# Keys and queries of a head pair by seven half-size products, with their copies behind the exponentials

## The chip, the cores and the metric

The kernel runs on one core of one Trainium2 chip. The metric is the device time of one execution in microseconds (us). All data are float32. The core's engines are TensorE (PE; its weight loads are shown apart as PEld), VectorE (DVE), ScalarE (ACT), GpSimd (POOL) and SyncE (SP, which here only issues DMAs). Each engine takes its instructions in the order of the program; semaphores hold an instruction back until what it needs is there.

## The reference, cut to what matters

Four sequences of 1024 rows and 256 features go through four layers, each added to its input:

```
x = x + attention_a(layernorm(x))      # layer 1: 16 heads of 64
x = x + ffn(layernorm(x))              # 256 -> 1024, exact gelu, -> 256
x = x + attention_b(layernorm(x))      # low-rank q, k, v and rotary embedding
x = x + ffn(layernorm(x))              # the same weights again
```

In layer 1, with `h = layernorm(x)` of one sequence, every head has

```
q, k, v = h @ Wq, h @ Wk, h @ Wv                 # 256 -> 64 each
scores  = (q @ k.T) / (64 * 64 * 16)
out     = softmax(scores) @ v                    # then out @ WO, summed over the heads
```

## The kernel before

**Pairs and steps.** Two heads make a pair (128 columns of a weight), so a sequence has 8 pairs and layer 1 has 32. A pair has 8 steps; a step handles 128 query rows of both heads against all 1024 keys. Layer 1 therefore has 256 steps, numbered `s`. Everything is written out by hand in the order in which the engines shall meet it: one pass of the loop in `steps_with` (L342 to L365) emits work of several steps, and `pieces` is a table that says after which pass other work (the projections of the next pair, layer norms, weight loads) is emitted. A key that ends in a half (`s - EARLY`) stands in the middle of the pass, between the two halves of a step's exponentials; a whole key stands at its end.

**One pass `s`.** In this order: `invert(s)` takes the reciprocal of the softmax sums (DVE, L268) and spreads it into an extra column block of `p` (ACT, L269). `scores(s + 1)` makes the scores of the next step: eight matmuls into two tiles `sc`, one for each half `j`, and the matmuls alternate between the tiles (L247). `exponentials(s + 1, j)` finds the row maximum of one `sc` tile (DVE, L258) and takes the exponential (ACT, L260); this is what reads `sc`. `turn(s)` transposes the probabilities in blocks of 32 (DVE, L280), and `send` carries the blocks to their places by DMA (L304, eleven by SP and five by POOL for two steps).

Passes come in twos. In a pass with odd `s` the kernel also multiplies the probabilities of two earlier steps with the values: `weigh` (PE, L313), then `take` copies the result (ACT, L323) and scales it (POOL, L325). In a pass with even `s` `project` multiplies that with the output weights (PE, L176 with `wo`, in `mm`), copies the sum out of PSUM (ACT, `got`, L335) and adds it to `x` (POOL, L337). Below, an even pass is called a projecting pass, an odd one a weighing pass, and both together a beat.

**The next pair's keys and queries.** While one pair's steps run, the next pair's are made. `qk` (L744 to L758) is called four times in a pair, once in each projecting pass, at a half key: for keys and queries, for each half of the sequence, it multiplies 128 weight columns with 512 columns of the transposed `hT`, over two chunks of the 256 features (`paired`: two column halves of PE for each chunk, so four matmuls a call, L176 with `hT,w`), and ACT copies the bank out (L756, L758), also between the step's two exponentials. `values` (L185, copied by L769) is called at the end of a projecting pass.

**PSUM.** It has eight banks. The pool `ps_sc` has three tiles of two banks, handed out in turn; in layer 1 only `scores` takes from it. The pool `ps_mm` has two tiles of one bank, taken alternately by everything else through `group`:

```
    ps_sc = ctx.enter_context(tc.tile_pool(name="ps_sc", bufs=3, space=PSUM))
    ps_mm = ctx.enter_context(tc.tile_pool(name="ps_mm", bufs=1, space=PSUM))
```

**Elsewhere.** Both feed-forward layers already multiply blocks by seven products instead of eight (`up_seven`, `down_seven`): sums of blocks are made first, the seven products are taken, and their results are added up. `w2_sb` (1 MB), and the rotary tables `cos_sb` and `sin_sb` (0.5 MB each), are loaded at the start on POOL's queue and stay in SBUF. `rows.measure` takes mean and variance of 128 rows on DVE (L135, L136); 24 such are spread over the steps 4 to 27, and the feed-forward layer's first eight over the steps 236 to 243.

Of the kernel before, what the change touches and what calls it, by code (L numbers as in the profile page):

```python
# [15 lines left out]
P = 128  # L16
# [3 lines left out]
NC = D // P  # L20
# [14 lines left out]
EPS = 1e-5  # L35
EARLY = 0.5
PLACES = {
    (3, 0): (0, 1), (3, 10): (2,), (3, 11): (3,), (3, 12): (4,), (3, 13): (5,),
# [10 lines left out]
def hybrid_block_kernel(  # L49
# [24 lines left out]
    pp, tp, ptp, otp, tmp = pool("p", 2), pool("T", 2), pool("pT", 2), pool("oT", 1), pool("tmp", 1)  # L74
    lowp, highp, xnp, rp = pool("low", 2), pool("high", 1), pool("xn", 1), pool("rope", 1)
    qkp, vp, wp, wop = pool("qk", 2), pool("v", 2), pool("wp", 2), pool("wo", 2)

# [15 lines left out]
    w1_sb = const.tile([P, NC, F], F32, name="w1_sb")  # L93
    w2_sb = const.tile([P, NF, D], F32, name="w2_sb")
    b2_sb = const.tile([P, D], F32, name="b2_sb")
    wd_sb = const.tile([P, 2, NC, P], F32, name="wd_sb")
    cos_sb = const.tile([P, S], F32, name="cos_sb")
    sin_sb = const.tile([P, S], F32, name="sin_sb")

    def load_rest():  # L100
        for b in range(1, B):
            nc.sync.dma_start(xs[b], xv[b])
        nc.gpsimd.dma_start(w1_sb, w1.rearrange("(c p) f -> p c f", p=P))
        nc.gpsimd.dma_start(w2_sb, w2.rearrange("(c p) d -> p c d", p=P))
        nc.gpsimd.dma_start(b2_sb, b2.partition_broadcast(P))
        for i, w in enumerate((wdq, wdkv)):
            nc.gpsimd.dma_start(wd_sb[:, i], w.rearrange("(c p) r -> p c r", p=P))
        for j in range(2):
            nc.gpsimd.dma_start(cos_sb[j * DH : (j + 1) * DH, :], rope_cos)
            nc.gpsimd.dma_start(sin_sb[j * DH : (j + 1) * DH, :], rope_sin)  # L110
        nc.gpsimd.dma_start(b1_sb, b1.rearrange("(c p) -> p c", p=P))
        nc.gpsimd.dma_start(lns_sb, ln_s.rearrange("(c p) -> p c", p=P))
        nc.gpsimd.dma_start(lnb_sb, ln_b.rearrange("(c p) -> p c", p=P))


# [41 lines left out]

    def transposed(dst, src, c, affine=None):

        tr = group(TQ, P)  # L160
        for t in range(TQ):
            nc.tensor.transpose(tr[:, t, :], src[:, t, ts(c, P)], ident)  # L162
        trf = tr.rearrange("p t q -> p (t q)")
        if affine is None:
            nc.scalar.copy(dst[:, c, :], trf)  # L165
        else:
            nc.scalar.activation(
                dst[:, c, :], trf, AF.Identity,
                scale=affine[0][:, c : c + 1], bias=affine[1][:, c : c + 1],
            )  # L170
# [18 lines left out]

    def attention(prep_batch, prep_pair, wo, loader, lead, kept):  # L190

# [135 lines left out]
        def project(h):  # L327
            g, t0 = divmod(HB * h, NT)
            b, pr = pairs[g]
            po = group(HB, D)  # L330
            for t in range(HB):
                paired(po[:, t, :], [(oT[h][:, t], [wos[g][:, t]] * 2)])
            oT.pop(h)
            got = tmp.tile([P, HB, D], F32, tag="tmp", name="got")
            nc.scalar.copy(got, po)  # L335
            xd = xs[b][:, t0 : t0 + HB, :]
            nc.gpsimd.tensor_add(xd, xd, got)  # L337

        def steps_with(others):
            for k, f in others:  # L340
                pieces.setdefault(k, []).append(f)
            for s in range(-1, n + LAG + 1):  # L342
                h, part = divmod(s - LAG, HB)
                ahead = 0 <= s + 1 < n
                if 0 <= s < n:
                    invert(s)
# [4 lines left out]
                if part == 1 and 0 <= h < n // HB:  # L351
                    project(h)
                if ahead:
# [5 lines left out]
                if ahead:  # L359
                    exponentials(s + 1, 1)  # L360
                if part == 0 and 0 <= h < n // HB:
                    take(h)
                if 0 <= s < n:
                    turn(s)
# [30 lines left out]
    def ffn(rows, store):  # L395
# [31 lines left out]
        def weights():  # L427
# [5 lines left out]
            parts["w1"] = (s1, w1_sb[:, 0, :m], w1_sb[:, 1, :m], w1_sb[:, 1, m:])  # L433
            lo, hi = w2_sb[:, :hf], w2_sb[:, hf:]
            parts["w2"] = (s2, lo[:, :, :P], hi[:, :, :P], hi[:, :, P:])
            v = nc.vector
            work = four([s1[:, i] for i in range(4)], w1_sb[:, 0, :m], w1_sb[:, 1, :m], w1_sb[:, 0, m:], w1_sb[:, 1, m:], [v] * 4)
            work += other([s2[:, i] for i in range(4)], lo[:, :, :P], lo[:, :, P:], hi[:, :, :P], hi[:, :, P:], [nc.gpsimd] * 4)
            for f in work:
# [114 lines left out]
        def down_seven(n, hook):  # L554
            b, qb = blocks[n]
            t4, b11, b21, b22 = parts["w2"]
            s, g = sums.pop(n), gT[n]
            a11, a12, a22 = g[:, :hf, :half], g[:, hf:, :half], g[:, hf:, half:]
            pairs = {
                1: (a11, b11), 2: (a12, b21), 3: (s[:, 3], b22), 4: (a22, t4[:, 3]),  # L560
                5: (s[:, 0], t4[:, 0]), 6: (s[:, 1], t4[:, 1]), 7: (s[:, 2], t4[:, 2]),
            }
# [4 lines left out]
            def product(bank, k, first):  # L567
                l, r = pairs[k]
                product_of(bank, lambda t, f: l[:, f, ts(t, P)], lambda f: r[:, f], first, hf)

# [39 lines left out]
        def down(n, t):  # L610
# [3 lines left out]
            for f in range(NF):  # L614
                nc.tensor.matmul(  # L615
                    po[n][:, t % 2, :], gT[n][:, f, ts(t, P)], w2_sb[:, f, :],
                    start=(f == 0), stop=(f == NF - 1),
                )
# [9 lines left out]
    def ffn_between(rows, store, n_steps, nxt=None, prologue=(), ramp=None):  # L628
# [11 lines left out]
        ends += [(n - 1 + (0, 0, 0, 1, 2, 2, 3, 3)[f], lambda f=f: up(0, f)) for f in range(NF)]  # L640
        ends += [(n, lambda: normed(1))]
        ends += [(n + 1, lambda m=m, t=t: rows.measure(m, t)) for m in range(2, 6) for t in range(TQ)]
        ends += [(n + 2, lambda: rows.finish[1]()), (n + 2, weights), (n + 3, lambda: turned(1))]
        ends += [(n + 3, lambda: row_sums(1)), (n + 4, lambda: down(0, 0))]

        def rest():
# [3 lines left out]
            for m in range(1, last + 1):  # L650
# [11 lines left out]
                if m == 1:  # L662
                    for i in range(2 * TQ):
                        when(2 + i, lambda i=i: rows.measure(6 + i // TQ, i % TQ))
                if nxt and m >= 2:
                    for t in range(TQ):
# [38 lines left out]
    def layer_a():  # L705

        scale_a = 1.0 / (DH * DH * H)
        hTs = {}
        rows = Rows("a", (blocks[:1], blocks[1:2], blocks[2:]))

        def batch_a(b):
            work = []
            for qb in range(NQB):
# [12 lines left out]
                def turned(c, b=b, k=k, qb=qb):  # L726
                    if c == 0:
                        p, tag = ((lowp, "low"), (highp, f"high{b % 2}"))[qb]
                        hTs[b, qb] = p.tile([P, NC, QB], F32, tag=tag, name="hT")
                    transposed(hTs[b, qb], k["xn"], c)  # L730

                work += [(10 * qb + t, lambda t=t, f=straight: f(t)) for t in range(TQ)]
                work += [(10 * qb + 6 + 2 * c, lambda c=c, f=turned: f(c)) for c in range(NC)]
            return work

        def pair_a(b, pr):
# [9 lines left out]
            def qk(i, qb):  # L746
# [6 lines left out]
                ])  # L753
                dst = made[name][:, ts(qb, QB)]
                if i == 0:
                    nc.scalar.mul(dst, pq, scale_a)  # L756
                else:
                    nc.scalar.copy(dst, pq)  # L758

            def values(m):  # L760
# [3 lines left out]
                for t in range(4):  # L764
# [3 lines left out]
                    ])  # L768
                nc.scalar.copy(made["v"][:, ts(m, 4), :], pv)  # L769

            work = [(4 - 4 * i + 2 * qb - EARLY, lambda i=i, qb=qb: qk(i, qb)) for i in (1, 0) for qb in range(NQB)]
            work += [(6 + 2 * m, lambda m=m: values(m)) for m in range(NT // 2)]
            return {name: lambda name=name: made[name] for name in ("qT", "kT", "v")}, load, work


        later = [(4 + i, lambda i=i: rows.measure(2 + i // TQ, i % TQ)) for i in range(6 * TQ)]
        later += [(4 + 6 * TQ, lambda: rows.finish[2]())]
        first, steps = attention(batch_a, pair_a, wo_a, nc.gpsimd, lead=3, kept=0)
        loads, xn, pair = first[:2], first[2:14], first[14:]
# [11 lines left out]
        first = loads + [lambda: measured(0)] + xn[:4] + [lambda: measured(1), ready] + xn[4:6] + pair[:1]  # L791
        first += xn[6:] + pair[1:3]
        later += [((-1, 0, 0, 1, 1)[i], f) for i, f in enumerate(pair[3:])]
# [3 lines left out]
    def layer_b(rows):  # L797
# [4 lines left out]
        def batch_b(b):  # L802
            work = []
            for qb in range(NQB):
# [33 lines left out]
                work += [(16 * qb - 12 + t, lambda t=t, f=second: f(t)) for t in range(TQ)]  # L838
                work += [(16 * qb - 8 + 2 * c - EARLY, lambda c=c, f=turned: f(c)) for c in range(NC)]
                work += [(16 * qb + 2 * m, lambda m=m, f=down: f(m)) for m in range(2)]  # L840
            return work

        def pair_b(b, pr):
# [23 lines left out]
            def rotate(i, qb):  # L867

                straight, other = made[i, qb], turned.pop((i, qb))
                nc.gpsimd.tensor_mul(straight, straight, cos_sb[:, ts(qb, QB)])  # L870
                nc.gpsimd.tensor_mul(other, other, sin_sb[:, ts(qb, QB)])  # L871
                nc.gpsimd.tensor_add(straight, straight, other)
# [19 lines left out]

        return attention(batch_b, pair_b, wo_b, nc.sync, lead=5, kept=1)

# [74 lines left out]
```

## Time and profile before

| what | value |
| --- | --- |
| median of 3 runs | 3253.63 us (3250.37 to 3256.33) |
| the profiled execution | 3250.15 us, its span 3248.4 us |
| granted clock of TensorE, mean | 0.996 |
| scores of layer 1 | 22.56 to 1412.5 us of the span; its last `weigh` until 1447.8 us |
| scores of layer 3 | 1661.0 to 3002.7 us; the feed-forward layers lie behind the two, overlapping their ends |

The profile is one execution as the hardware profiler saw it. Busy shares are averages over these four stages, so layer 1 is read by itself, from a stretch of steady steps. Times in a timeline are us from the start of the span; a number in square brackets is how long the engine was idle before an instruction, with what it waited for.

### The profile page before, as it was taken

Reading aid. Unit: us, or ns where it says so; the run is one execution under the profiler, and the core shown is the slowest. Engines: PE = TensorE matmul, PEld = TensorE weight load, DVE = VectorE, ACT = ScalarE, POOL = GpSimd, SP = SyncE. Lnnn points to the kernel's source line nnn. Section 1 sums busy time; section 2 is a strip of 40 time slices with the busy share of each in tenths; the row PEclk is TensorE's granted clock in tenths of the full one; section 3 lists DMA queues with packets and bytes.
Section 4 is the critical chain, followed back from the end, with each engine's and each line's share of the span. In section 5 each row is a group of like instructions: output and inputs, shape, how many; then the busy total and the mean of one; then the engine's idle time right before and its main releaser. Section 6 shows DMA issues by size and latency. Waiting matters only on the chain.

```text
span 3248.4 us, 128967 instructions
## 1 busy us (share of the span) xinstructions
PE 3164.4 (97%) x53648; PEld 2092.2 (64%) x53648; DVE 2723.5 (84%) x2686; ACT 2137.9 (66%) x4400; POOL 2002.1 (62%) x2782
## 2 busy tenths in 40 slices
PE   8999999999999999999999999999999999999999
PEld 4666666666666666668866566666666666655688
DVE  7988888888888888966569989998999999999554
ACT  5666666666666666655447777777778777777542
POOL 4544545455444545442249889899899889886311
PEclk9999999999999999999999999999999999999999
DMA  8888888888888888850029889988989899988200
GB/s 228 217 224 215 224 224 228 217 219 222 221 217 225 219 231 223 221 150 1 4 74 244 225 228 243 242 237 236 246 243 243 234 240 246 238 235 221 57 20 27
DMA packets 244709, 642.29 MB, mean 198 GB/s; under 512 B 74304, under 2 KB 102976, under 8 KB 244128
## 3 DMA queue, kind: packets, MB, share of 16 engines
q1 hardware_dynamic: 161104, 397.60, 48.0%
q0 software_dynamic: 83024, 236.44, 26.0%
q8 instruction: 426, 6.98, 1.0%
q14 instruction: 155, 1.27, 0.1%
HBM read 43.39 MB, written 4.19 MB: 15 GB/s over the span
## 4 chain that ended last, share of the span: by engine, by line
PE 69%; SPq 12%; DMA 6%; DVE 5%; ACT 4%; issue 3%; POOL 1%; DVEq 0%; ACTq 0%; POOLq 0%
PE sc L247 20%; PE mm L313 19%; PE mm L176 15%; SPq L304 11%; DMA pT<-T 5%; PE pw L495 4%; PE mm L185 4%; PE mm L495 3%; PE mm L615 2%; DVE T L280 2%; DVE nmax L258 1%; ACT p L260 1%; PE ph L604 1%; ACT gT L529 1%; PE mm L162 1%
## 5 line engine op out<-in xcount | busy, mean ns | idle before, releaser
L258 DVE TENSOR_REDUCE nmax<-sc 128x1 f32<-128x1024 f32 x1024 | 1204.5, 1218 | 214.3 <-PE sc L247 211.3
L260 ACT ACTIVATE p<-sc,nmax 128x1024 f32<-128x1024 f32 x1024 | 1145.3, 1119 | 322.3 <-DVE nmax L258 322.2
L280 DVE STREAM_TRANSPOSE T<-p 128x2176 f32<-128x2176 f32 x512 | 1247.3, 2436 | 48.4 <-DMA pT<-T 18.4
L247 PE MATMUL sc<-kT,qT 64*64 64x512 f32 x8192 | 1082.5, 598 | 11.9 <-ACT p L260 10.3
L313 PEld LDWEIGHTS mm<-pT,v 64*64 64x64 f32 x32768 | 949.5, 133 | 140.7 <-issue 98.5
L313 PE MATMUL mm<-pT,v 64*64 64x128 f32 x32768 | 983.0, 269 | 9.6 <-issue 8.5
L304 POOL DMA_DIRECT2D pT<-T x1280 | 629.6, 499 | 125.5 <-PE sc L247 57.7
L325 POOL TENSOR_TENSOR oT<-oT,pT 128x256 f32<-128x256 f32 x256 | 187.0, 730 | 696.3 <-ACT oT L323 623.0
L247 PEld LDWEIGHTS sc<-kT,qT 64*64 64x64 f32 x8192 | 332.8, 133 | 401.6 <-issue 274.5
L337 POOL TENSOR_TENSOR x<-x,got 128x512 f32<-128x512 f32 x256 | 331.0, 1293 | 25.8 <-ACT got L335 22.0
L335 ACT COPY got<-mm 128x512 f32<-128x512 f32 x256 | 150.0, 586 | 281.8 <-PE mm L176 281.8
L176 PE MATMUL mm<-wo,oT 128*64 128x256 f32 x2048 | 279.9, 394 | 24.1 <-POOL oT L325 22.8
L176 PEld LDWEIGHTS mm<-wo,oT 128*64 128x64 f32 x2048 | 124.9, 136 | 273.2 <-POOL oT L325 226.5
L269 ACT COPY p<-total 128x128 f32<-128x128 f32 x512 | 151.9, 297 | 198.6 <-DVE total L268 192.4
L176 PE MATMUL mm<-hT,w 128*64 128x512 f32 x1024 | 243.4, 597 | 0.9 <-ACT hT L165 0.9
L260 ACT ACTIVATION_READ_ACCUMULATOR p<-sc,nmax 128x1 f32 x1024 | 205.2, 200 | 0.0
L185 PEld LDWEIGHTS mm<-w,hT 128*64 128x64 f32 x4096 | 140.9, 138 | 71.3 <-issue 69.4
L871 POOL TENSOR_TENSOR turned<-turned,sin_sb 128x512 f32<-128x512 f32 x128 | 163.8, 1279 | 0.0
L409 POOL TENSOR_TENSOR x<-x,b_sb 128x256 f32<-128x256 f32 x64 | 48.8, 777 | 170.6 <-ACT xn L156 170.6
L296 ACT COPY pT<-T 32x1088 f32<-32x1088 f32 x128 | 140.3, 1096 | 4.9 <-DMA pT<-T 1.1
L185 PE MATMUL mm<-w,hT 128*64 128x64 f32 x4096 | 140.9, 222 | 0.2 <-ACT kT L758 0.2
L176 PEld LDWEIGHTS mm<-hT,w 128*64 128x64 f32 x1024 | 73.3, 138 | 96.8 <-issue 75.0
(145 smaller groups left out, 2928.5 us busy)
## 6 DMA issues: line engine op xcount, KB each, us to landing
pT<-T SPq DMA_DIRECT2D x2688, 136.0 KB, 4.7
pT<-T POOLq DMA_DIRECT2D x1280, 136.0 KB, 4.7
turned<-kT POOLq DMA_DIRECT2D x128, 128.0 KB, 3.4
turned<-qT POOLq DMA_DIRECT2D x128, 128.0 KB, 3.5
w<-in_wqkv_a POOLq DMA_DIRECT2D x96, 128.0 KB, 6.0
wo<-in_wo_a POOLq DMA_DIRECT2D x32, 128.0 KB, 5.4
wo<-in_wo_a POOLq DMA_DIRECT2D x64, 64.0 KB, 5.5
wo<-in_wo_b SPq DMA_DIRECT2D x32, 128.0 KB, 4.0
```

What stands on the lines that cost most here:

```text
L176: nc.tensor.matmul(out[ts(j, DH)], lhsT[:, ts(j, DH)], rhs[j], start=(first and i == 0), stop=(last and i == len(parts) - 1),)
L185: nc.tensor.matmul(out[ts(j, DH)], lhsT, rhs[:, ts(j, DH)], start=(i == 0), stop=(i == len(parts) - 1),)
L247: nc.tensor.matmul(sc[s, j][ts(half, DH), ts(m, 512)], qT()[rows, ts(2 * qs + half, DH)], kT()[rows, ts(m, 512)], start=True, stop=True,)
L258: nc.vector.tensor_reduce(nmax, sc[s, j], AX.X, ALU.max, negate=True)
L260: nc.scalar.activation(probs[s][:, :NK2, ts(j, 2), :], sc.pop((s, j)).rearrange("p (k c i) -> p k c i", c=2, i=SQ), AF.Exp, bias=nmax, acc ...
L280: nc.vector.transpose(T[h][:, :, q, :, :].rearrange("p c k i -> p k c i"), probs.pop(s))
L304: engine.dma_start(pT[h][ts(c, SQ), a], T[h][ts(a, SQ), c])
L313: nc.tensor.matmul(av[h][q][ts(j ^ q, DH)], v[ts(j, DH), k, :], pT[h][ts(j, DH), :, q, k, :], start=(k == 0), stop=(k == NK2 - 1),)
L325: nc.gpsimd.tensor_mul(parts, parts, pT.pop(h)[:, :, :, NK2, :])
L337: nc.gpsimd.tensor_add(xd, xd, got)
L495: nc.tensor.matmul(bank[:, t, : right(k).shape[-1]], left(t, k), right(k), start=(first and t == 0 and k == 0), stop=(k == n_k - 1), skip_ ...
L871: nc.gpsimd.tensor_mul(other, other, sin_sb[:, ts(qb, QB)])
```

## The change

The keys and queries of a pair, for one sequence, are a product of 2 by 2 blocks: queries and keys as rows, the two feature chunks as the inner index, the two halves of the sequence as columns. That took eight block products; now it takes seven (numbered 1 to 7), for 31 of the 32 pairs. The first pair still calls `qk`.

Before the products, POOL makes four sums of weight blocks of a pair (`weight_sums`, at a key two passes before the pair's first products), and DVE makes four differences of blocks of `hT` once for each sequence (`row_sums`: for the first sequence ahead of the first step, for the other three in the passes 21 to 24 after their table's zero). The products are taken in the four projecting passes in the groups (1, 6), (7, 5), (4, 2) and (3), each group into one `ps_sc` tile of two banks, tag `sc`. At the end of the pass ACT copies one product of the group, and DVE and POOL add: DVE one sum out of PSUM in each of the first three groups, POOL none, two, one and one sums in SBUF.

With `late=True` (layer 1 only) `project` returns its copy and addition, and they are emitted after the step's second exponential, unless more than one piece of that pass takes a `ps_mm` bank (`banked`). The scale of the scores moves into the copy of `hT` (`root`), and `values` undoes it. To make room in SBUF, `w2` is loaded in four parts at the end of layer 1 and the rotary tables in the first feed-forward layer, both on SP's queue; their space (pool `tail`) serves the sums before.

```diff
@@ def project(h):
-            got = tmp.tile([P, HB, D], F32, tag="tmp", name="got")
-            nc.scalar.copy(got, po)
-            xd = xs[b][:, t0 : t0 + HB, :]
-            nc.gpsimd.tensor_add(xd, xd, got)
+            def added():
+                got = tmp.tile([P, HB, D], F32, tag="tmp", name="got")
+                nc.scalar.copy(got, po)
+                xd = xs[b][:, t0 : t0 + HB, :]
+                nc.gpsimd.tensor_add(xd, xd, got)
+
+            return added
@@ one pass
                 if part == 1 and 0 <= h < n // HB:
-                    project(h)
+                    added = project(h)
+                    both = pieces.get(s - EARLY, []) + pieces.get(s, [])
+                    if not late or sum(getattr(f, "banks", 0) for f in both) > 1:
+                        added()
+                        added = None
...
                 if ahead:
                     exponentials(s + 1, 1)
+                if added:
+                    added()
@@ def pair_a(b, pr):
+            def weight_sums():
+
+                s = made["s"] = tail.tile([P, 4, P], F32, tag="w20", name="ws")
+                (q0, q1), (k0, k1) = [[made["w"][:, i, c, :] for c in range(NC)] for i in range(2)]
+                nc.gpsimd.tensor_add(s[:, 0], k0, k1)
+                nc.gpsimd.tensor_sub(s[:, 1], s[:, 0], q0)
+                nc.gpsimd.tensor_sub(s[:, 2], q0, k0)
+                nc.gpsimd.tensor_sub(s[:, 3], q1, s[:, 1])
+
+            def products(which):
+
+
+                w, s, t = made["w"], made["s"], [sums[b][k // 2][:, k % 2] for k in range(4)]
+                h = [[hTs[b, qb][:, c, :] for qb in range(NQB)] for c in range(NC)]
+                sides = {
+                    1: (w[:, 0, 0], h[0][0]), 2: (w[:, 0, 1], h[1][0]), 3: (s[:, 3], h[1][1]),
+                    4: (w[:, 1, 1], t[3]), 5: (s[:, 0], t[0]), 6: (s[:, 1], t[1]), 7: (s[:, 2], t[2]),
+                }
+                both = ps_sc.tile([P, 2, QB], F32, tag="sc", name="pw")
+                for i, k in enumerate(which):
+                    made[k] = both[:, i]
+                for k in which:
+                    l, r = sides[k]
+                    paired(made[k], [(l, [r] * 2)])
+
+            def added(which):
+
+
+                q, k = made.get("qT"), made.get("kT")
+                if which == (1, 6):
+                    made["u2"] = tail.tile([P, QB], F32, tag="w22", name="u2")
+                    nc.vector.tensor_add(made["u2"], made[6], made["x1"])
+                elif which == (7, 5):
+                    made["u3"] = tail.tile([P, QB], F32, tag="w23", name="u3")
+                    nc.vector.tensor_add(made["u3"], made[7], made["u2"])
+                    nc.gpsimd.tensor_add(made["u2"], made["u2"], k[:, QB:])
+                    nc.gpsimd.tensor_add(k[:, QB:], k[:, QB:], made["u3"])
+                elif which == (4, 2):
+                    nc.vector.tensor_add(k[:, :QB], made[4], made["u3"])
+                    nc.gpsimd.tensor_add(q[:, :QB], q[:, :QB], made["x1"])
+                else:
+                    nc.gpsimd.tensor_add(q[:, QB:], q[:, QB:], made["u2"])
...
-            work = [(4 - 4 * i + 2 * qb - EARLY, lambda i=i, qb=qb: qk(i, qb)) for i in (1, 0) for qb in range(NQB)]
-            work += [(6 + 2 * m, lambda m=m: values(m)) for m in range(NT // 2)]
+            if b == 0 and pr == 0:
+                work = [(0, lambda i=i, qb=qb: qk(i, qb)) for i in (1, 0) for qb in range(NQB)]
+            else:
+                work = [(-2, weight_sums)]
+                for i, which in enumerate(((1, 6), (7, 5), (4, 2), (3,))):
+                    work += [(2 * i - EARLY, lambda which=which: products(which))]
+                    work += [(2 * i, lambda which=which: copied(which))]
+                    work += [(2 * i, lambda which=which: added(which))]
+            work += [(6 + 2 * m, banked(lambda m=m: values(m))) for m in range(NT // 2)]
```

The function `copied` (not shown) holds the ACT copy of each group: of product 1 into `x1`, of 5 into the keys, of 2 and of 3 into the queries.

## The prediction

> **What bounds the kernel now.** I read the page first, then layer 1 by itself, because the busy shares are averages over four stages.
>
> ```profile
> PE 3164.4 (97%) x53648; PEld 2092.2 (64%) x53648; DVE 2723.5 (84%) x2686; ACT 2137.9 (66%) x4400; POOL 2002.1 (62%) x2782
> ```
>
> PE is busy almost throughout. Whether that means "full" is seen in the chain that ended last, for a stretch of layer 1 (start, us, what): one beat, from the end of one projecting pass's scores to the end of the next one's.
>
> ```profile
> 608.01 2.73 PE mm L176 x16
> 610.74 0.93 PE mm L185 x32
> 611.67 1.88 PE sc L247 x16
> 613.55 3.49 PE mm L313 x128
> 617.04 1.72 PE sc L247 x16
> ```
>
> Nothing but PE stands in it, without a gap: 2.73 + 0.93 + 1.88 + 3.49 + 1.72 = 10.75 us. (L176 holds the projection and `qk` together.) So layer 1 is bound by PE's matmuls, and taking some away can help, if nothing else is close behind. What is close behind is seen in the timeline of the same beat.
>
> ```profile
> 608.06 2.36 DVE L258 TENSOR_REDUCE nmax<-sc 128x1 f32<-128x1024 f32 x2 [0.46 <-PE sc L247]
> 608.85 1.89 PE L176 MATMUL mm<-hT,w 128*64 128x512 f32 x8
> 609.12 0.59 ACT L335 COPY got<-mm 128x512 f32<-128x512 f32 x1 [1.19 <-PE mm L176]
> 609.61 1.12 ACT L260 ACTIVATE p<-sc,nmax 128x1024 f32<-128x1024 f32 x1
> 610.33 2.44 DVE L280 STREAM_TRANSPOSE T<-p 128x2176 f32<-128x2176 f32 x1
> 611.27 1.12 ACT L260 ACTIVATE p<-sc,nmax 128x1024 f32<-128x1024 f32 x1
> 611.60 0.21 PEld L247 LDWEIGHTS sc<-kT,qT 64*64 64x64 f32 x8
> 613.60 2.36 DVE L258 TENSOR_REDUCE nmax<-sc 128x1 f32<-128x1024 f32 x2 [0.78 <-PE sc L247]
> ...
> 615.99 1.12 ACT L260 ACTIVATE p<-sc,nmax 128x1024 f32<-128x1024 f32 x1
> ...
> 617.00 0.19 ACT L260 ACTIVATION_READ_ACCUMULATOR p<-sc,nmax 128x1 f32 x1
> ```
>
> DVE idles only 0.46 + 0.78 = 1.24 us in a beat. And the scores of the weighing pass start at 611.60, while the projecting pass's second exponential still runs (to 612.39). They may, because with three `sc` tiles in turn they take the third tile and the first.
>
> **Part 1, the matmul removed.** Of 2.73 us in the chain the projection has 0.85 (the weighing pass ends the same way), `qk` 1.88: four matmuls, that is two block products of 0.94 us. Groups (1, 6), (7, 5), (4, 2) stay at 1.88; group (3) saves 0.94. If PE's work set the time: 31 pairs × 0.94 = 29 us less. A rule of the Trainium skill speaks otherwise ("Perfetto Trace Analysis", Identifying the Most-Contended Engine: judge TensorE's headroom by its weight loads, not by matmul busy time): by it PEld's 64% would leave room and this term would be worth about 0. The gapless chain is against that, so I go by the row.
>
> **Part 2, the tile taken from the scores.** A group of products takes one of the three `sc` tiles in every projecting pass. Then the turn is: scores X, Y; products Z; scores of the weighing pass X, Y again. These now need *both* exponentials of the step just before. The copies of `got` and of the product move behind the second exponential, which brings that one forward; I work out when it ends. In the weighing pass, where no copy stands between, the reductions start at 613.60 and the second exponential's last instruction ends at 617.00 + 0.19 = 617.19, so 3.59 after. For reductions at 608.06: 611.65. The release costs little more; the layer's first steps show it, where the scores do wait:
>
> ```profile
> 26.83 0.19 ACT L260 ACTIVATION_READ_ACCUMULATOR p<-sc,nmax 128x1 f32 x1
> 26.95 1.11 ACT L260 ACTIVATE p<-sc,nmax 128x1024 f32<-128x1024 f32 x1
> 27.07 0.28 PEld L247 LDWEIGHTS sc<-kT,qT 64*64 64x64 f32 x8 [0.58 <-ACT p L260]
> ...
> 29.06 2.35 DVE L258 TENSOR_REDUCE nmax<-sc 128x1 f32<-128x1024 f32 x2 [0.70 <-PE sc L247]
> ```
>
> Released at 27.02, weights at 27.07, and the next reduction 1.99 after that, as in the free case (611.60 to 613.60). The first matmul, which goes into the first tile, had run alone before, and that saved nothing. So in the beat above the scores can go on at 611.70 instead of 611.60, and the loop closes on itself: reductions to release 3.64, release to the next reductions 1.99, weighing and scores to the next projecting pass's reductions (613.60 to 618.81) 5.21: 10.84 us a beat against 10.75. PE's own work no longer enters. In the group (3) beat PE comes 0.94 earlier and waits 0.94 + 0.09. The whole gain of part 1 is spent, and 31 × 4 beats × 0.09 = **+11 us** come on top.
>
> **Part 3, DVE's additions.** Three a pair; the nearest row is the feed-forward's sum out of PSUM:
>
> ```profile
> L540 DVE TENSOR_TENSOR u<-pw,u 128x512 f32<-128x512 f32 x14 | 9.5, 675 | 0.7
> ```
>
> 0.68 us each, placed after the transpose. In the order of instructions each waits for ACT's product copy too. ACT: exponential to 611.65, then `got`, `v`, the copy (0.59, 0.37, 0.59, each starting some 0.1 before the last one's shown end): to about 613.0. The addition then runs to 613.75, the reciprocal to 613.85, and the reductions start there instead of at 613.70. Behind them come the exponentials, `take` (POOL at 617.64 + 0.25, 0.73 long, to 618.62) and the projection, which starts at 618.69 today. It just fits: +0.02 a beat, **+3 us**. If ACT's copies follow more slowly by 0.2, it is 0.2 on 93 beats, 19 us.
>
> **Part 4, beats where DVE has no room.** 32 measures (385 + 182 ns) fall two to a beat into 16 beats: 1.13 of the slack of 1.24. With an addition, 0.68 + 1.13 less the new slack of 1.24 + 0.09 = 1.33 is 0.5 us over in three quarters of them: +6. The 12 block differences of the later sequences come two to a beat in six beats, 0.69 each (the feed-forward's 128x512 difference of weights took 693 ns): up to 0.7 over, +3. Together **+9**, from 3 to 20. The Trainium skill ("SBUF — State Buffer", Who interferes with whom) says that a DVE instruction with both inputs in SBUF and a GpSimd one that reads SBUF block each other for a whole instruction. A similar sum that took 1100 ns instead of 680 agrees with something like it; with a full block of 1.29 us for each of the 12 the term would be some 15 us larger. The additions of part 3 have one input in PSUM and are outside that rule.
>
> **Part 5, POOL.** Additions of 128x512 take 1.29 us (L337), 128x256 0.73 (L325), so 128x128 about 0.45 by that slope (estimate). Group (7, 5): `got` 612.3 to 613.6, two additions to 616.2, before `take` at 617.6: hidden. The tight beat is group (3): `got` 613.6, one addition 614.9, four weight sums 616.7, then the three `wo` loads (0.58 + 2 × 0.53) 618.3, and only then `take`, to 619.1: the projection starts 0.3 late, of which 0.1 was waiting anyway: 31 × 0.2 = **+6**, from 0 to 10. Group (4, 2) has one addition and three `w` loads (2.2 us) to 617.1: hidden by 0.5.
>
> **Part 6, the ends.** In the first six steps, where reductions come every 4.65 us (DVE sets the pace), three additions come in: +2. The first sequence's four differences fall into DVE's idle 11.49 us before its first reduction: 0. 2 MB fewer loads in the first 30 us: 0, as PE waits there for ACT and DVE, not for loads; at most 2.1 MB at the 293 GB/s of that window, −7. The later loads (eight issues on SP's queue, about 1 us each) delay transfers that lag five steps: 0. The scale in the copies (598 ns with, 587 without) and POOL's split weight sums in the feed-forward layers: 0. **+2**, from −7 to 5.
>
> **Sum.** 11 + 3 + 9 + 6 + 2 = +31 on the profiled execution's 3250.15: 3281. That execution lies 3.5 under the median of the runs, within their spread of 6; I say 3281. One measurement of this kernel can tell about 0.2% (6.5 us) from no change.
>
> **Rivals.**
>
> *The gain comes through (faster).* The scores' wait decides only if the second exponential is released later than PE arrives. If it ended 0.94 us earlier in the group (3) beats than worked out (by 610.66), 29 us come off, less the small terms (10): 3231. For it: ACT has 34% idle. Against it: 608.06 + 3.59 is two reductions and one exponential in a row, without any idle time to take out. I give it 0.10.
>
> *All fits, no change.* Parts 3 to 5 vanish in slack, the start gives a few us back: 11 − 7 = +4, 3254. It needs the projection's start, today 0.31 after POOL's end, to absorb everything. 0.15.
>
> *DVE becomes the bound.* If addition, copy wait and semaphores take 0.3 more per beat than the 1.33 of slack, in all 93 beats with an addition: +28 on top, 3309. For it: 9.5 busy of 10.75 before, 10.2 after. 0.20.
>
> *The forecast*, waits a little longer than PE's work: 0.55.
>
> The products are taken in 31 of 32 pairs by the order of instructions, so "it does nothing" is no case.
>
> **Range.** Low 3252, with the waits at 0.09 and nearly all else hidden; high 3314, with DVE as the bound. The faster case and the tails are left out. Faster 0.10; same 0.13, since the case of no change reaches a little past the bound; slower the rest, 0.77.
>
> **What would show it.** Right: in layer 1 PE idle before L266 (the scores' new line), released by ACT `p`, about 1 us once a pair; DVE's idle time before the reductions nearly gone; beats of 10.85 to 11.1. Part 5 is right if the projection after group (3) waits for POOL `oT`. Wrong: beats of 10.75 with one of 9.8 in each pair; or PE waiting for something else, such as the weights' sums or DMA.

## The result, and the profile after

The changed kernel takes 3268.02 us (median of 20 runs, 3261.26 to 3279.43) against 3253.43 (20 runs, 3247.26 to 3262.66). The ratio is 1.0044, 95% interval 1.0036 to 1.0052: slower by 14.6 us. Forecast were 3281 and a range from 3252 to 3314. The profiled execution took 3261.26 us with a span of 3259.5, that is 11.1 more than before's; the runs and traces of one kernel differ by several us, so the loss is located by layer below.

The page's first part: the shares of PE and ACT stay, DVE and POOL gain the sums.

```profile
PE 3171.1 (97%) x53524; PEld 2129.3 (65%) x53524; DVE 2800.6 (86%) x2795; ACT 2132.6 (65%) x4400; POOL 2206.5 (68%) x3033
```

Now the timeline of two beats of layer 1. The first has group (4, 2), the second group (3); L277 are the reductions, L279 the exponentials, L266 the scores, L356 is `got`, L862 DVE's addition.

```profile
625.09 2.35 DVE L277 TENSOR_REDUCE nmax<-sc 128x1 f32<-128x1024 f32 x2 [0.46 <-PE sc L266]
626.34 1.11 ACT L279 ACTIVATE p<-sc,nmax 128x1024 f32<-128x1024 f32 x1 [1.39 <-DVE nmax L277]
...
628.49 0.19 ACT L279 ACTIVATION_READ_ACCUMULATOR p<-sc,nmax 128x1 f32 x1
628.58 0.57 ACT L356 COPY got<-mm 128x512 f32<-128x512 f32 x1
628.63 0.30 PEld L266 LDWEIGHTS sc<-kT,qT 64*64 64x64 f32 x8
...
629.95 0.69 DVE L862 TENSOR_TENSOR kT<-pw,u 128x512 f32<-128x512 f32 x1 [0.16 <-ACT qT L845]
...
630.72 2.36 DVE L277 TENSOR_REDUCE nmax<-sc 128x1 f32<-128x1024 f32 x2
...
635.92 2.36 DVE L277 TENSOR_REDUCE nmax<-sc 128x1 f32<-128x1024 f32 x2 [0.46 <-PE sc L266]
...
638.62 0.19 PEld L266 LDWEIGHTS sc<-kT,qT 64*64 64x64 f32 x2
639.33 0.19 ACT L279 ACTIVATION_READ_ACCUMULATOR p<-sc,nmax 128x1 f32 x1
...
639.57 0.21 PEld L266 LDWEIGHTS sc<-kT,qT 64*64 64x64 f32 x8 [0.77 <-ACT p L279]
```

The first beat lasts from 625.09 to 635.92: 10.83 us, where it was 10.75. In the second beat PE, with one product fewer, comes to the scores at 638.62 and loads the weights of the first matmul. Then it stands until 639.57, 0.05 us behind the end of the second exponential's last instruction (639.33 + 0.19). The matmul taken away has turned into a wait for the exponential. Over a long stretch of layer 1 (100 to 1300 us) the waits say the same (who waited for what: us, times, longest):

```profile
DVE nmax L277 <- PE sc L266: 70.1, 125, 1.5
...
PEld mm L332 <- issue: 36.4, 150, 0.8
PEld sc L266 <- ACT p L279: 25.1, 41, 1.5
```

Of these 25.1 us, 19.9 lie in the 27 group (3) passes of the stretch, 0.74 a pair (0.77 in most). Two weight loads go ahead of each such wait, 0.19 us in the lines above: in that beat PE is 639.57 − 638.62 = 0.95 us early, the time of one block product (0.94).

All beats can be measured: the starts of DVE's reductions, read from the timeline, give 256 steps, and a beat is the distance over two of them. This table has the 102 beats that begin in the passes 32 to 234, by the group of products taken in them (before: by the call of `qk` in the same place): median, and mean behind the stroke. The last column is layer 1 from the second step's reductions to the last step's.

| kernel | (1, 6) | (7, 5) | (4, 2) | (3) | layer 1, us |
| --- | --- | --- | --- | --- | --- |
| before | 10.75 / 10.97 | 10.75 / 10.88 | 10.75 / 10.78 | 10.75 / 11.01 | 1384.1 |
| after | 11.09 / 11.25 | 10.84 / 10.95 | 10.84 / 10.88 | 10.84 / 11.09 | 1401.8 |
| after, unaltered, in a later job (`e9_again`) | 11.08 / 11.28 | 10.84 / 10.94 | 10.84 / 10.92 | 10.84 / 11.11 | 1402.7 |

So layer 1 is 17.7 to 18.6 us longer. The order of layer 3's work is the same in all these kernels, but the way from its first step to its last took from 1330.9 to 1347.4 us in the eleven traces; with that spread the rest of the kernel shows neither gain nor loss.

### The profile page after: what moved, and what is told of

It reads as the page before. It is cut to its first block, busy times and chain, and to the rows that moved or that the text cites. A ratio compares the mean times of both kernels' runs of the same rounds, so it can differ in the third digit from the quotient of the medians.

```text
span 3259.5 us, 129216 instructions
## 1 busy us (share of the span) xinstructions
PE 3171.1 (97%) x53524; PEld 2129.3 (65%) x53524; DVE 2800.6 (86%) x2795; ACT 2132.6 (65%) x4400; POOL 2206.5 (68%) x3033
## 4 chain that ended last, share of the span: by engine, by line
PE 61%; SPq 16%; DMA 7%; DVE 6%; ACT 4%; issue 4%; POOL 2%; DVEq 0%; ACTq 0%; POOLq 0%
PE sc L266 18%; PE mm L332 16%; SPq L323 15%; PE mm L190 8%; DMA pT<-T 6%; PE pw L190 5%; PE pw L532 4%; PE mm L199 4%; PE mm L532 3%; DVE nmax L277 2%; DVE T L299 2%; PE mm L653 2%; ACT p L279 1%; PE ph L642 1%; POOL oT L344 1%
## 5 line engine op out<-in xcount | busy, mean ns | idle before, releaser
L279 ACT ACTIVATE p<-sc,nmax 128x1024 f32<-128x1024 f32 x1024 | 1143.4, 1117 | 413.5 <-DVE nmax L277 413.5
L277 DVE TENSOR_REDUCE nmax<-sc 128x1 f32<-128x1024 f32 x1024 | 1203.7, 1217 | 145.0 <-PE sc L266 142.3
L266 PE MATMUL sc<-kT,qT 64*64 64x512 f32 x8192 | 1139.3, 599 | 16.6 <-ACT p L279 13.7
L332 PEld LDWEIGHTS mm<-pT,v 64*64 64x64 f32 x32768 | 972.4, 133 | 125.3 <-issue 94.8
L332 PE MATMUL mm<-pT,v 64*64 64x128 f32 x32768 | 1013.0, 269 | 7.6 <-issue 4.4
L266 PEld LDWEIGHTS sc<-kT,qT 64*64 64x64 f32 x8192 | 380.4, 133 | 407.5 <-issue 247.7
L356 ACT COPY got<-mm 128x512 f32<-128x512 f32 x256 | 148.7, 581 | 146.2 <-PE mm L190 146.2
L279 ACT ACTIVATION_READ_ACCUMULATOR p<-sc,nmax 128x1 f32 x1024 | 202.9, 198 | 0.0
L985 POOL TENSOR_TENSOR turned<-turned,sin 128x512 f32<-128x512 f32 x128 | 163.8, 1280 | 0.0
L190 PE MATMUL mm<-hc,w 128*64 128x512 f32 x512 | 133.3, 597 | 0.0
L342 ACT COPY oT<-mm 128x128 f32<-128x128 f32 x512 | 110.2, 267 | 10.3 <-PE mm L332 9.6
```

The costliest lines, as they stand in the source:

```text
L190: nc.tensor.matmul(out[ts(j, DH)], lhsT[:, ts(j, DH)], rhs[j], start=(first and i == 0), stop=(last and i == len(parts) - 1),)
L266: nc.tensor.matmul(sc[s, j][ts(half, DH), ts(m, 512)], qT()[rows, ts(2 * qs + half, DH)], kT()[rows, ts(m, 512)], start=True, stop=True,)
L277: nc.vector.tensor_reduce(nmax, sc[s, j], AX.X, ALU.max, negate=True)
L279: nc.scalar.activation(probs[s][:, :NK2, ts(j, 2), :], sc.pop((s, j)).rearrange("p (k c i) -> p k c i", c=2, i=SQ), AF.Exp, bias=nmax, acc ...
L332: nc.tensor.matmul(av[h][q][ts(j ^ q, DH)], v[ts(j, DH), k, :], pT[h][ts(j, DH), :, q, k, :], start=(k == 0), stop=(k == NK2 - 1),)
L985: nc.gpsimd.tensor_mul(other, other, held["sin"][:, ts(qb, QB)])
```

## The experiments

The theory was that of the prediction: the products' tile makes the weighing pass's scores wait for the second exponential, so a beat is 10.84 us whatever PE has to do. Its rivals were that PE's own work, DVE's additions or POOL's queue set the time. Medians of the kernel before on the chips of the three jobs were 3251.0, 3252.9 and 3250.82; ratios are against these.

### The tile alone

```diff
-                pq = group(QB)
+                made[i, qb] = ps_sc.tile([P, 2, QB], F32, tag="sc", name="pw")[:, 0]
```

with the copy at the end of the pass, and none of the sums. The later copy of `got` and the moved loads stay as in the changed kernel.

> The eight products of qk as before, without any sums on DVE and POOL, but each bank is taken from the score tiles, and its copy and got stand behind the second exponential as in the changed kernel. Theory: the tile alone lengthens each beat from 10.75 to 10.84 (31 x 4 x 0.09), 11 us more than the kernel before: 3264. Rival (the sums on DVE and POOL are the whole loss): the time of the kernel before, 3253.

3256.17, ratio 1.0016 (1.0007 to 1.0026). The beats:

| kernel | (1, 6) | (7, 5) | (4, 2) | (3) | layer 1, us |
| --- | --- | --- | --- | --- | --- |
| `e3_tile_alone` | 10.84 / 11.04 | 10.84 / 10.94 | 10.84 / 10.89 | 10.84 / 11.01 | 1393.9 |

PE takes the eight products of before, and the median beat has its 0.09 us more in every group: 9.8 us in layer 1 by the trace, where 11 were expected. By the medians of the runs it is 5.2 us (2 to 9 by the interval), nearer to the rival's 0 than to the 11, in kernels whose other layers vary by more than that; the beats decide between the two. The tile with the later copies is shown as this part of the loss, without the sums; the later copies without the tile were not run. That is a little more than half of the 18; the rest is not the tile.

### Product 3 twice

```diff
-                    paired(made[k], [(l, [r] * 2)])
+                    for _ in range(2 if which == (3,) else 1):
+                        paired(made[k], [(l, [r] * 2)])
```

> Product 3 is taken twice into the same bank, so PE does as many block products as before (eight). Theory: PE stands idle about 1 us in that beat, the second taking falls into it, and the time stays within 3 us of the changed kernel's 3268. Rival (PE's own work still sets the beat and the loss lies elsewhere): 31 x 0.94 = 29 us more, 3297.

3269.96, ratio 1.0056 (1.0043 to 1.0068); layer 1 1406.2, so 4 us more than after (by the trace, and by the medians, each against the kernel before in its own job), not 29. The group (3) beat has a median of 10.91. The waits of 100 to 1300 us show where the second taking went:

```profile
PEld sc L266 <- ACT p L279: 4.0, 12, 1.5
```

25.1 us of waiting became 4.0, and in the group (3) passes 19.9 became 0.2. An eighth product is nearly free here: PE's work does not set the beat.

### Product 3 in a bank of the other pool

```diff
+                if which == (3,):
+                    both = group(1, QB)
+                else:
...
+                    work += [(2 * i - EARLY, banked(f) if which == (3,) else f)]
```

> Product 3, which is alone in its group, goes into a one-bank tile of the other PSUM pool (as qk's bank did), so in this one beat of a pair no score tile is taken. Its pass then copies got early, by the kernel's own rule. Theory (the reused score tile makes the scores wait for the second exponential, and this eats the 0.94 us of PE that group (3) saves): the scores now wait for the first exponential only, that beat falls from 10.84 to about 10.0 us (release 2.81 after the reductions, 1.99, 5.21), so 20 to 26 us less than the changed kernel, about 3245, below the kernel before. Rival (DVE's additions or POOL fill the beat): the beat stays above 10.6 and the time within 5 us of the changed kernel's 3268.

3258.03, ratio 1.0024 (1.0013 to 1.0035): 10 us less than the changed kernel's 3268, and 8 less when each is set against the kernel before in its own job, where 20 to 26 were expected. With no score tile taken, 10 of the 25 beats of group (3) are 10.19 to 10.21 us long, so the wait is gone as the theory has it. Its timeline:

```profile
725.98 2.36 DVE L277 TENSOR_REDUCE nmax<-sc 128x1 f32<-128x1024 f32 x2 [0.46 <-PE sc L266]
...
727.05 0.58 ACT L356 COPY got<-mm 128x512 f32<-128x512 f32 x1 [1.20 <-PE mm L190]
...
727.69 1.01 PEld L199 LDWEIGHTS mm<-w,hT 128*64 128x64 f32 x32 [0.76 <-ACT got L356]
728.51 2.44 DVE L299 STREAM_TRANSPOSE T<-p 128x2176 f32<-128x2176 f32 x1 [0.17 <-DMA pT<-T]
...
728.77 0.23 PEld L266 LDWEIGHTS sc<-kT,qT 64*64 64x64 f32 x8
...
730.92 2.33 DVE L277 TENSOR_REDUCE nmax<-sc 128x1 f32<-128x1024 f32 x2
...
736.17 2.36 DVE L277 TENSOR_REDUCE nmax<-sc 128x1 f32<-128x1024 f32 x2 [0.52 <-PE sc L266]
```

The scores start at 728.77, while the second exponential runs. What ends last now is DVE, which goes from reductions to transpose, reciprocal and reductions with one wait of 0.17 us, for a DMA (725.98 to 730.92, 4.94 us). But 9 of the 25 beats are above 11.3 us, so the mean of group (3) is still 10.85, and the group (1, 6) beat behind has a median of 11.04 and a mean of 11.38, against 11.25 in the changed kernel. Layer 1 takes 1397.3 us, 4.5 less than after.

### The loads of `wo` two passes later

```diff
-            pieces.setdefault(NT * g - 1 - EARLY, []).append(lambda g=g: load_out(g))
+            pieces.setdefault(NT * g + (1 if late and g else -1) - EARLY, []).append(lambda g=g: load_out(g))
```

> The changed kernel with the three loads of wo two passes later on POOL's queue, so that they no longer stand between the weight sums and the take that the projection behind group (3) waits for. Theory (POOL's queue behind group (3) delays that projection by 0.2 to 0.3 us): the beat of group (1, 6) falls from 11.09 to 10.84 us, 31 x 0.25 = 8 us less than the changed kernel, 3260. Rival (that beat is long for DVE's sake, which waits there for the copy of product 1): no change, 3268.

3269.23, ratio 1.0058 (1.0044 to 1.0071): no gain. The beats of group (1, 6) do shorten:

| kernel | (1, 6) | (7, 5) | (4, 2) | (3) | layer 1, us |
| --- | --- | --- | --- | --- | --- |
| `e4_wo_later` | 10.86 / 11.08 | 10.85 / 11.00 | 10.84 / 10.94 | 10.84 / 11.05 | 1398.2 |

The median of the changed kernel, 11.09, was the length of no beat: 13 of its 26 beats of group (1, 6) take 10.84 to 10.97 us, the next 11.19. A delay of over a microsecond behind group (3) is there in two of the 26; the chain in the changed kernel shows one (start, us, what), from the loads over `take` to the projection:

```profile
645.62 0.58 POOL wo L240
646.20 0.11 POOL wo L242
...
646.71 0.53 POOL wo L242
647.25 0.75 POOL oT L344
648.00 0.04 issue
648.04 1.08 PE mm L190 x8
```

In this beat POOL had also stood 2.74 us before two of its transfers, for nothing that the profile shows; in the other, 2.79 us before three. With the loads moved the same two waits are there (2.75 and 2.79 us), but the projection is no longer late, and the two beats, 12.74 and 12.18 us in the changed kernel, take 11.35 and 10.84. That is 2.7 us of the 3.6 by which layer 1 is shorter. The timed runs don't show it: against the kernel before in its own job this version loses 18.2 us, the changed kernel 14.6.

### `got` ahead of the exponentials

```diff
-        first, steps = attention(batch_a, pair_a, wo_a, nc.gpsimd, lead=3, kept=0, late=True)
+        first, steps = attention(batch_a, pair_a, wo_a, nc.gpsimd, lead=3, kept=0, late=False)
```

> The changed kernel, but got is copied and added where it was before, ahead of the step's exponentials (the products' copies stay behind them). Theory (the second exponential's end sets the beat): got's copy puts the exponentials of the projecting pass back by about 0.4 us, and each of 124 beats becomes that much longer: 45 to 50 us more than the changed kernel, about 3315. Rival (ACT has a third of its time idle, the place of a copy does not matter): 3268.

3285.59, ratio 1.0108 (1.0093 to 1.0122), 17.6 us more than the changed kernel; medians of 11.11 us in all four groups, layer 1 1421.1. The direction is the theory's, the size a little over a third. In the timeline the reductions start at 713.60 and the scores are released here:

```profile
717.25 0.21 ACT L279 ACTIVATION_READ_ACCUMULATOR p<-sc,nmax 128x1 f32 x1
717.51 0.25 PEld L266 LDWEIGHTS sc<-kT,qT 64*64 64x64 f32 x7 [0.18 <-ACT p L279]
```

3.86 us after the reductions instead of 3.59: 0.27 later, not 0.4, since `got` starts before the first maximum is there and puts only a part of itself in front. In the group (1, 6) beats the mean rises by 0.09 alone. Those with transpositions had `got` early already, and in three, which hold one of DVE's block differences, POOL's addition of `got` is over sooner and the difference takes 0.64 to 0.65 us instead of 1.34 to 2.23 (more on this in part 4 below).

### Two of DVE's three additions left out

```diff
-                    nc.vector.tensor_add(made["u2"], made[6], made["x1"])
+                    made["u2"] = made["x1"]
...
-                    nc.vector.tensor_add(made["u3"], made[7], made["u2"])
+                    made["u3"] = made["x1"]
```

> Two of DVE's three additions of a pair (the sums of products 6 and 7, L855 and L858) are left out, and what reads them takes the copy of product 1 instead, so keys and queries are not the reference's. Theory (DVE's additions fit into its idle time, except in the few beats with measures or block differences): 2 to 6 us less than the changed kernel, and beats of 10.84 us stay. Rival (DVE is the bound): 20 us or more less.

3263.9, ratio 1.0041 (1.0029 to 1.0054), 4 us less by the medians; layer 1 1401.0, 0.8 less in the trace. The beats of (7, 5) and (4, 2) stay at 10.84. DVE is not the bound.

### Both repairs, and one more

> Product 3 into a bank of the other PSUM pool and the three wo loads two passes later, both together. Theory: with POOL's queue free behind group (3), the beat of group (3) falls to 10.0 to 10.2 us and that of group (1, 6) to 10.84 to 10.9, 15 to 25 us less than the changed kernel in layer 1, 3243 to 3253, at or below the kernel before. Rival (the transfers through SP's queue, or DVE, now set the pace of these beats): no better than product 3 in its bank alone, 3258.

3261.2, ratio 1.0029 (1.0016 to 1.0041): no better than product 3 in its bank alone. The short beats come (15 of 25 in group (3) at 10.18 to 10.30; the group (1, 6) median is 10.84), layer 1 falls to 1390.2. But 10 beats of group (3) take 10.87 to 12.52 us. In three of them PE waited 1.5 us for the copy of product 3 before it could transpose, since both take the same pool's banks; three hold two block differences each (11.36 to 11.78); in two others PE stopped for 1.5 us in the middle of the weighing, for nothing that the profile shows. One of these, in the timeline (the 1.51 of the matmuls, the 1.75 of the loads ahead of them):

```profile
995.53 0.30 PEld L332 LDWEIGHTS mm<-pT,v 64*64 64x64 f32 x9 [1.75 <-issue]
995.53 0.54 PE L332 MATMUL mm<-pT,v 64*64 64x128 f32 x9 [1.51 <-issue]
```

So one more version moves the transpositions:

```diff
-                work += [(10 * qb + 6 + 2 * c, banked(lambda c=c, f=turned: f(c))) for c in range(NC)]
+                work += [(((4, 8), (16, 18))[qb][c], banked(lambda c=c, f=turned: f(c))) for c in range(NC)]
```

> As the kernel with product 3 in its bank and wo two passes later, with one transposition of each later sequence (two pieces of the four) moved from group (3)'s pass to that of group (4, 2), and one from (1, 6) stays: the three beats where PE waited for the copy of product 3 before transposing (12.2 to 12.5 us) fall to about 11.4. Theory: 3 to 4 us less than without the move, some 10 us less than the changed kernel. Rival (what the short beats gain is given back elsewhere, by the supply of instructions or transfers): no difference.

3257.83, ratio 1.0019 (1.0009 to 1.0030). The three beats fall to 10.19 to 10.21 us, further than the expected 11.4, and layer 1 is 2.7 us shorter than without the move. On the same chip the changed kernel took again 3265.7, ratio 1.0045 (1.0033 to 1.0058):

> The changed kernel unaltered, on the same chip as the run beside it, so that the two are compared directly: 3268, or 14 us more than the kernel before.

| kernel | (1, 6) | (7, 5) | (4, 2) | (3) | layer 1, us |
| --- | --- | --- | --- | --- | --- |
| `e8_no_clash` | 10.84 / 11.12 | 10.84 / 11.01 | 10.85 / 11.04 | 10.20 / 10.55 | 1387.5 |

8 us less than the changed kernel, a little under the expected 10, and still 7 more than before. By the means of the beats, the fourth one now saves 11.01 − 10.55 = 0.46 us against before, 31 × 0.46 = 14 us. The other three lose 0.15 + 0.13 + 0.26 = 0.54, 31 × 0.54 = 17 us, of which 31 × 3 × 0.09 = 8 is the tile and the rest are long beats, those with block differences among them. That is 3 us more in layer 1, which measures 1387.5 − 1384.1 = 3.4. No version tried beats the kernel before.

## Why the prediction was right, point by point

**The bound and part 1.** Before, PE's matmuls set layer 1, and the change took 0.94 us a pair off them: both hold. That the removed matmul is worth something only where nothing else holds the beat is seen in the 10.19 us beats of the version with product 3 in its bank. The Trainium skill ("Perfetto Trace Analysis", Identifying the Most-Contended Engine) judges TensorE's headroom by MFU and by the busy share of its weight loads; read by PEld's 64% alone, PE would have had room before and this term would be 0. The runs speak for the row of the chain: with the tile set free, the beat without the product is 0.55 us shorter than the one of before.

**Part 2, the tile.** Forecast: 3.64 to the release, 1.99 to the next reductions, 5.21 to the following ones, 10.84 a beat, also for group (3), where PE waits about 1 us. Measured: 10.84 in the median of three groups, 5.63 + 5.21; in group (3) PE comes 0.95 us early in the beat shown, and its waits there add up to 0.74 a pair. For the tile by itself 9.8 us in the trace of layer 1 and 5.2 by the medians, instead of 11. This is the step that decided the sign.

**Part 3, DVE's additions.** Each took 0.69 us (0.68 forecast) and waited some 0.15 for ACT's copy; they fit, a little better than forecast (+3): leaving two out gave 0.8 us in the trace of layer 1 and 4 by the medians.

**Part 4, beats without room: mis-sized.** +9 was forecast. From step 9 to step 33, where most of the measures fall, layer 1 lost 2.4 and 2.3 us against before in the two traces of the changed kernel, and 1.4 with the tile alone. So about 1 us is left for the measures, not the +6 of the forecast; they do not fill DVE as tightly as the sum assumed. The block differences cost more than the +3 forecast. They do not fall two to a beat into six beats, but one, two and one into the beats of groups (4, 2), (3) and (1, 6), three times in the layer, nine beats. Together these nine are 5.3 us longer than nine of 10.84 in one trace of the changed kernel and 6.3 in the other, 0.1 with the tile alone. Most of the twelve differences took longer than the 0.69 assumed:

```profile
L788 DVE TENSOR_TENSOR hs<-hT,hs 128x512 f32<-128x512 f32 x6 | 8.6, 1436 | 0.0
L788 DVE TENSOR_TENSOR hs<-hT 128x512 f32<-128x512 f32 x6 | 5.9, 975 | 0.0
...
333.26 1.27 POOL L358 TENSOR_TENSOR x<-x,got 128x512 f32<-128x512 f32 x1 [1.55 <-ACT got L356]
333.74 1.34 DVE L788 TENSOR_TENSOR hs<-hT,hs 128x512 f32<-128x512 f32 x1
```

The Trainium skill ("SBUF — State Buffer", Who interferes with whom) says that a DVE instruction with both inputs in SBUF contends with a GpSimd one that reads SBUF. The traces agree. The difference shown ends at 335.08, 0.55 us after POOL's addition (334.53). In the nine traces that have them there are 144 differences; 87 took more than 0.70 us, up to 2.23, and each of the 87 ends 0.54 to 0.57 us after a POOL operation on SBUF tiles (an addition, or `take`) beside it has ended. The other 57 took 0.64 to 0.70. So a difference waits until POOL's operation is over, in 84 of the 87 for the rest of one that had begun before; twelve full blocks, which the prediction put at 15 us, are too many (the two rows above are 6.2 us over twelve of 0.69). Where POOL's addition came sooner (`got` ahead of the exponentials), the differences of three beats were back at 0.64 to 0.65.

**Part 5, POOL: near in number, by luck.** +6 was forecast, the projection behind group (3) 0.2 us late in each of 31 pairs. In most beats it starts 0.04 us before the reductions, where it starts 0.11 before them with `wo` later; those 0.07 us cost nothing, since the scores wait for the second exponential anyway. In two of the 26 beats it is more than 1.2 us late, and these are 1.40 and 1.34 us longer than with the tile alone: 2.7 us. That the mean of group (1, 6) rose by 11.25 − 10.97 = 0.28, less the tile's 0.09, and that 0.19 × 31 = 6 us agrees with the forecast, is chance: most of the rise comes from those two beats and from the three with a block difference.

**Part 6.** The second reductions came at 28.33 us instead of 29.06 (27.92 in the other trace): −0.7 and −1.1 at the start, where 0 was forecast. From there to step 9 layer 1 lost 1.9 us in one trace of the changed kernel and 0.9 in the other, where +2 was forecast. But with the tile alone, without any of the additions, it also lost 1.9, so the additions are not shown to be what cost there.

**The sum.** In layer 1, 11 + 3 + 9 + 6 + 2 = 31 were forecast and 18 measured. The measured parts are the tile (9.8), the beats with block differences (5.3) and the two late projections (2.7), 17.8 of 17.7 us; in the other trace 9.8 + 6.3 + 2.7 = 18.8 of 18.6; what the remaining beats gain and lose against the tile alone nearly cancels. The sign and the mechanism of part 2 are as forecast, the size is not: too large were the measures (6 for about 1), part 5 (6 for 2.7) and part 3 (3 for about 1), too small the block differences (3 for 5.3). The median over all runs, 14.6, lies another 3 below, within what the layers behind vary by, and is a little under half of the 31. The rival "the gain comes through" needed the second exponential 0.94 us earlier; it ended where the rows put it. "DVE becomes the bound" was wrong by the kernel without two additions. "All fits" would have come near only without the tile's part and the block differences.

## What to carry to other kernels

Before work is taken from the engine that bounds a loop, write down the next loop behind it with its own length: here reductions, second exponential, scores, weighing, 10.84 us, was 0.09 longer than PE's 10.75 as soon as the products borrowed the tile that had let the scores run ahead. A PSUM buffer that looks free can be what decouples two engines, and its price can be tested by itself, by borrowing it without the rest of the change. When a repair shortens a beat and the total does not follow, compare means with medians: the median shows the mechanism, the mean what is given back. Then list the beats one by one: where they fall into two groups, as those of group (1, 6) did, the median may be the length of none, and a mean that agrees with a forecast can come from a few long beats with other causes.

## What the runs showed of the hardware

Three things were not expected. A DVE subtraction of 128x512 with both inputs in SBUF took 0.64 to 0.70 us in 57 of 144 cases, and in the other 87 ended 0.54 to 0.57 us after an operation of POOL beside it. Where POOL came second, in four cases, its operation took 0.8 to 1.26 us instead of 0.46 to 0.74. In the repaired kernels PE stopped in the middle of a weighing for 1.5 us (its weight loads for 1.75), in one beat of `e8_no_clash` for 1.78, waiting for nothing that the profile shows (one is in the lines above; before, PE's own longest such idle time from 100 to 1300 us was 0.8 us). Whether this is the supply of instructions was not tried. And layer 3, whose order of work is unchanged, varied by 16.5 us between traces, as much as the effect studied, so that a single span could not have placed the loss, while the beats of layer 1 agree to 0.01 us in their medians.
